# Graph layer on one Trainium2 core: where the first ranks, the first equality matrices, the early loads and the last list stand in a hand-ordered schedule

## Chip, cores and metric

The kernel runs on 1 core of one Trainium2 chip. The metric is the device time in microseconds (us) of one execution.

## The reference

200000 edges with 20 features each join 6250 nodes with 128 features. Cut to what is computed:

```python
h = relu(layernorm(x))                                   # 6250 x 128
xn = h @ W_in
W_ij = (softplus(f_ij @ W_f1 + b_f1) - log 2) @ W_f2 + b_f2   # one row for each edge
x_ij = xn[dst] * (W_ij * edge_weight1)                   # dst is sorted, src is not
out = segment_sum(x_ij, src, 6250)
return x + (softplus(out @ W_o1 + b_o1) - log 2) @ W_o2 + b_o2
```

The gather index (dst) is sorted, so neighbouring edges read neighbouring rows. The index of the sum (src) is not.

## The kernel before

The edges are cut into 391 quads of 512 edges. One quad is one **item** of the loop at line 1361. For each item PE multiplies the features (`s1_pe`, tile z), ACT takes exponential and logarithm (`s1_exp`, line 379, and `s1_ln`), DVE makes a one-hot matrix of the relative rows (`s1_oh`, line 391, from the tile rb, for two quads at a time), PE gathers node rows with it (`s2_pe_x`) and multiplies the second weights (`s2_pe_w`), ACT scales (`s2_copy`, line 572) and DVE multiplies the two (`s2_m`, line 582). Features are split into three bf16 parts on the chip, a block `fB[b]` of 4096 edges at a time (`fb_load`, `fb_1` to `fb_4`, and `fb_max`, which takes the block's largest value), and written to the DRAM tensor fsd. `load_sc(s)` reads ft from there for quads 2s and 2s+1, beside rb and the node rows wn. ft, rb and wn are loaded about four items ahead.

The products are summed by src in one of three ways:

- **Plain** quads (197 are not sorted; the first 12 of them and the last are plain): `s1_eq` compares the quad's src with itself into the tile eq, PE adds up equal rows with it (`s3_pe`), and four indirect DMAs with accumulation (**scatters**, line 644, issued by POOL) add the rows to an accumulator in DRAM. There are four accumulators, acc0 to acc3; `acc_of(k)` says which one scatter k goes to.
- **Listed** quads (the other unsorted ones): rows go out by scatters directly; rows whose src appears twice in a chunk are sent to rows of a list instead, and a window of 16 quads has one list of 128 rows. For each window, `l_eq`, `l_count` to `l_take` prepare the indices from tiles sb (four buffers); at its end `l_load` reads the list's rows from all four accumulators, `l_sum` (line 531) adds up equal ones on PE, and one scatter sends them.
- **Sorted** quads (every second item, 2, 4, ... 388): edges get a rank among those with the same 1/16 of the nodes (`rank_group` to `rank_slot`, eight quads at a time), one-hot matrices pm (`perm_oh`) permute the product's bf16 parts on PE (`permute`), ACT takes them to the tile sg (`perm_out`, line 766), SP sends sg into the tiles mst in another layout (`regroup`, line 773), and some items later **units** of 8 or 10 quads (`unit`, matmuls un of line 863) add them to accT, the transposed sums of all nodes in SBUF. `unit_evac` (line 879) adds PSUM to accT. What does not fit goes by an overflow row (`over_...`) with a scatter of its own.

eq and sg share one tag of three buffers. Each engine does its instructions in program order, and the order is written out by hand: `at(i, point, fn)` hangs a function on a point of item i, and the points (L, D0, D1, AX, DM, DR, PE2, D2, S and others) are run in the order of the loop's body. `put` takes offset and point from the table `AT`. SP issues most DMAs, also in this order.

Ahead of the loop stands a **prologue**: node group 0, block 0, items 0 and 1 whole, then `consts_late` (constants of the ranks, of the lists and of the overflow rows). Accumulators are zeroed in ten pieces each (`zero_piece`): acc0 and acc1 by POOL in the prologue, acc2 by SP in items 0 to 3 (Z2), acc3 by SP in items 14 to 41 (Z3). The second half of the relative rows is made by `half_load` and `half_piece` in items 1 to 5; items from 196 on read it.

Units are at items 24, 28, 32, 36, 40 and so on; the last four at 395, 397, 399 and 401. The last list starts at item 394 (`l_start`, then `over_row`, `l_load`, `l_sum`). Behind the loop come a check of flags, and a tail (lines 1511 to 1617) that reads acc1 to acc3, adds them and accT, and does the last two matrix products.

Of the kernel before, what the change touches and what calls it, by code (L numbers as in the profile page):

```python
# [7 lines left out]
F32 = mybir.dt.float32  # L8
BF16 = mybir.dt.bfloat16
I32 = mybir.dt.int32  # L10
# [3 lines left out]
ALU = mybir.AluOpType  # L14
AX = mybir.AxisListType
# [5 lines left out]
P = 128  # L21
SC = 1024
SEG = 512
# [46 lines left out]
CQ = 16  # L70
EARLY_N = 256
ZMAX = 60.0


@with_exitstack
def tile_gnn(ctx: ExitStack, tc: tile.TileContext, x, fB, cT, srcT, srcr, srci, dstr, win_, wf1, wf2, bias, bo1c, wo1,
# [20 lines left out]
    GN = NP // GRP  # L97
    ZR = 10 if ACC_R % 10 == 0 else 1
    ZEARLY = 3
    K1_END, K2_END, K3_END = 0, 12, 100  # L100
    Z2, Z3 = [0, 1, 1, 2, 2, 3, 3, 3, 3, 3], range(14, 44, 3)
    mpq = sorted_quads(NQ)
    mpi = {q: n for n, q in enumerate(mpq)}
    rounds = unit_rounds(mpq)
# [216 lines left out]
        fst[b]["f3"] = f3  # L321

    def fb_max(b):
        nc.vector.tensor_reduce(fmax[:, b:b + 1], fst[b]["f"], axis=AX.X, op=ALU.max, apply_absolute_value=True)

    def fb_2(b):
        fr = wk.tile([P, FE], F32, tag="fr", name="fr", bufs=1)
# [6 lines left out]
    def fb_4(b):  # L334
        f3 = fst[b]["f3"]
        nc.vector.tensor_tensor(f3[:, 2], fst[b]["fr"], f3[:, 1], op=ALU.subtract)
        nc.sync.dma_start(fsd[b].rearrange("g (p e) -> p g e", p=P), f3)
        del fst[b]

    def seg_of(s):  # L340
        return SEG if spread and s < HALF else WSEG
# [64 lines left out]
    def s1_eq(q):  # L406
        if not plainq(q):
            return
        n = plain[q]
        eq = wk.tile([P, 4, P], F32, tag="eq", name="eq", bufs=3)  # L410
        v = sbs[n // 2][:, n % 2 * SEG:(n % 2 + 1) * SEG]
        for b in range(2):
            nc.vector.tensor_tensor(eq[:, 2 * b:2 * b + 2],
                                    v[:, 2 * b * P:2 * (b + 1) * P].rearrange("p (i t) -> p t i", t=2),
                                    srcT_sb[:, n * 4 + 2 * b:n * 4 + 2 * b + 2].unsqueeze(2).to_broadcast([P, 2, P]),
                                    op=ALU.is_equal)
        st[q]["eq"] = eq
# [151 lines left out]
    def s2_copy(q):  # L569
        xc = wk.tile([P, 4, P], F32, tag="xc", name="xc")  # L570
        for c in range(4):
            nc.scalar.mul(xc[:, c, :], st[q]["xg"][:, c, :], late["c", q // CQ][:, 4 * (q % CQ) + c:4 * (q % CQ) + c + 1])  # L572
        st[q]["xc"] = xc

    def s2_m(q):
        if q in mpi:
            m = part_new(q)
        elif plainq(q):
            m = ms[plain[q] % 2]
        else:  # L580
            m = sp_.tile([P, 4, 132], F32, tag="s", name="s", bufs=6)
        nc.vector.tensor_tensor(m[:, :, :P], st[q]["W"], st[q]["xc"], op=ALU.mult)  # L582
        st[q]["m"] = m
# [82 lines left out]
    def rank_local(r):  # L666
        nc4 = rk[r]["n"]
        ext = exts[r % 2]
        nc.vector.scalar_tensor_tensor(ext[:, :nc4, 1], rk[r]["cnt"], float(-GN), rk[r]["srcf"], op0=ALU.mult,
                                       op1=ALU.add)  # L670
        nc.scalar.copy(ext[:, :nc4, 2], rk[r]["cnt"])
        rk[r]["ext"] = ext
# [254 lines left out]
    with tc.manual_schedule():  # L927
# [96 lines left out]
        iotl = cp.tile([P, P + LCAP], F16, name="iotl")  # L1024

        def consts_late():
            nc.vector.tensor_reduce(fmax[:, 0:1], fb0, axis=AX.X, op=ALU.max, apply_absolute_value=True)
            nc.vector.memset(onesf, 1.0)
            nc.vector.memset(dropT, 0.0)
            for ext_ in exts:  # L1030
                nc.vector.memset(ext_, 0.0)
            nc.vector.tensor_copy(wgtb, wgt)
            nc.vector.tensor_scalar(tri, iot[:, :P], lane, None, op0=ALU.is_gt)
            nc.vector.tensor_scalar(unit2[:, 0], iot[:, :P], lane, None, op0=ALU.is_equal)
            nc.vector.tensor_scalar(unit2[:, 1], iot[:, :P], lane, float(GN), op0=ALU.is_equal, op1=ALU.mult)
            nc.vector.tensor_scalar(trib, iot[:, :P], lane, float(BIG), op0=ALU.is_equal, op1=ALU.mult)
            nc.vector.tensor_tensor(trib, trib, tri, op=ALU.add)
            nc.vector.tensor_scalar(iotp, iot, float(BIG), None, op0=ALU.add)
            for mo_ in mos:
                nc.vector.tensor_copy(mo_[:, PW:PW + 1], wgt)  # L1040
            nc.vector.tensor_scalar(iotl, iotw[:, GN // 2:GN // 2 + P + LCAP], float(LCAP - 1), None, op0=ALU.subtract)
# [12 lines left out]
        def at(i, point, fn, *a):  # L1054
            hooks.setdefault((i, point), []).append((fn, a))

        def put(name, base, fn, *a, busy=()):
            d, point = AT[name]
            i = max(clear(base + d, busy) if busy else base + d, 0)
            at(i, point, fn, *a)  # L1060
            return i
# [2 lines left out]
            for fn, a in hooks.pop((i, point), []):  # L1064
                fn(*a)

        at(2 if spread else 0, "D2", rel_ext, 0, rel0)
        if CE < EP // P:
            w = (CE + 4 * NS) // 2
            for i, a, b in ((8, CE, w), (10, w, 4 * NS), (13, CB, EP // P)):  # L1070
# [4 lines left out]
            at(CQ * b - CQ // 2, "L", c_load, b)  # L1075

        def half_load(k):
            t_ = pg.tile([HALF, SEG], I32, tag="pm", name="half")
            nc.sync.dma_start(t_, dstr[HALF:2 * HALF, k * SEG:(k + 1) * SEG])
            idx[1, k * SEG] = t_  # L1080

# [2 lines left out]
            rel_ext(1 + k, rel(1, lo, hi, "x3", bufs=1))  # L1084

        for k in range(2):
            at(k + 1 if spread else 0, "L", half_load, k)
            at(2 * k + 3 if spread else 0, "D2", half_piece, k)
        for j in range(ZR):
            at(Z2[j] if spread else 0, "L", zero_piece, nc.sync, 2, j)  # L1090
        for j in range(ZR):
# [20 lines left out]
        for b in range(1, NB):  # L1112
            t0 = 2
            if b > 1:
                t0 = 8 * b - 8
                while t0 + 1 not in mpi or t0 + 1 in units:
                    t0 -= 1
                at(max(0, t0 - 6), "L", fb_load, b)
            if b > 1:
                put("fmax", t0, fb_max, b)  # L1120
            else:
                at(2, "D2", fb_max, b)
            put("f1", t0, fb_1, b)
            put("f2", t0, fb_2, b)
            put("f3", t0, fb_3, b)
            put("f4", t0, fb_4, b)
# [112 lines left out]
        for g in range(len(tgroups)):  # L1239
# [2 lines left out]
            at(i - 2, "L", r0_load, g)  # L1242
            at(i, "PE2", r0_tp, g)
            at(i + 1, "D0", r0_add, g)
        for r in range(-(-len(mpq) // RKQ)):
            i = mpq[RKQ * r]
            early = i < 8
            i = max(i, 4)
            put("rk_group", i, rank_group, r)
            put("rk_local", i, rank_local, r)  # L1250
            k = put("rk_count", i, rank_count, r, busy=units)
            k = max(k + 1, i + AT["rk_own"][0])
            at(k, AT["rk_own"][1], rank_own, r)
            k = clear(max(k, i + AT["rk_over"][0]), units)
            at(k, AT["rk_over"][1], rank_over, r)
            k = max(k + 1, i + AT["rk_slot"][0])
            assert k <= i + 1
            at(k, AT["rk_slot"][1], rank_slot, r)
# [3 lines left out]
        for w in range(NW):  # L1262
            for g in range(wsize[w] // 4):
                n = LB + SW * (w - 1) + 4 * g - LSHIFT
                i = splain[n] + 2 if w else 6 + 2 * g
                while w and (i not in mpi or i in units):
                    i -= 1
                for k in range(2):
                    kk = (LB + SW * w + 4 * g) // 2 + k
                    at(max(0, i + k - 2), "L", sb_load, kk)  # L1270
                    put("l_eq", i + k, l_eq, kk)
                i = put("l_count", i, l_count, (LB + SW * w) // 4 + g, busy=units)
                k = put("l_dup", i, l_dup, w, g)
            i = put("l_scan", i, l_scan, w)
            i = put("l_before", i - 1, l_before, w, busy=units)
            put("l_index", i, l_index, w)
            assert i + 1 <= splain[LB + SW * w] + 1
            put("l_id", i, l_id, w)
            i = put("l_place", i, l_place, w, busy=units)
            put("l_take", i, l_take, w)  # L1280
            i = clear(wend[w] + wlag[w], units)
            at(i, "L", l_start, w)
            put("l_dg", i, l_dg, w)
            at(i, "PE2", over_row, ("L", w))
            put("l_same", i, l_same, w)
            k = clear(i + AT["l_sum"][0], units)
            at(k - 1, "L", l_load, w)
            at(k, AT["l_sum"][1], l_sum, w)
            put("l_copy", k, l_copy, w)
            put("l_ji", k, l_ji, w)  # L1290
            k = put("l_int", k, over_int, ("L", w))
            at(k, "S", over_scatter, ("L", w))
# [51 lines left out]
            s1_ln(q)  # L1344
            s1_oh(q)
        for q in range(first):
            s1_eq(q)
            s2_pe_x(q)
            s2_pe_w(q)
            s2_copy(q)  # L1350
            s2_m(q)
        for q in range(first):
            s3_pe(q)
            s3_copy(q, 0)
            s3_copy(q, 1)
            s3_idx(q)
            s3_ji(q)
            s3_scatter(q)
        consts_late()
        s1_pe(first)  # L1360
        for i in range(max(NQ + 7, last + 22, r0_end + 2, lend + 24)):
            if i % 2 == 0 and i // 2 + 2 <= (NQ - 1) // 2:
# [301 lines left out]
def clear(i, busy, n=1):  # L1664
    while any(i + k in busy for k in range(n)):
        i += 1
    return i
# [114 lines left out]
```

## Time and profile before

| what | us |
|---|---|
| median of 3 runs | 1887.07 |
| lowest and highest of them | 1877.03, 1892.61 |
| the profiled execution | 1900.09 |
| its span | 1898.3 |
| mean granted TensorE clock, as a share of full speed | 0.963 |

Times in the profile count from the span's start. PE is TensorE's matmuls, PEld its weight loads, DVE VectorE, ACT ScalarE, POOL GpSimd, SP the engine that issues DMAs; SPq is its queue. A line of the timeline gives start, duration, engine, line of the kernel, operation, output and input, a count, and in brackets how long the engine had been idle and what ended that. A line of the waits gives who waited for whom: total, number of times, longest. Releasers are inferred.

### The profile page before, as it was taken

To read this page: it belongs to the slowest core of one execution; us is meant where nothing else is said; L and a number is where in the kernel's file an instruction comes from. 1 tells how busy PE (TensorE), PEld (TensorE's weight loads), DVE (VectorE), ACT (ScalarE), POOL (GpSimd) and SP (SyncE) were. 2 spreads that over 40 slices of the span, in tenths; PEclk is the share of its full clock that TensorE was granted. 3 is DMA by queue.
4 is the path that set the end of the run, shared out by engine and by line. 5 is a ranking of instruction groups with operands and counts; after the bars stand their busy time and mean duration, and the time that the engine had idled before them with its cause. 6 is when DMAs were issued, how large, how long until landed. Compare 5 with 4: busy or idle time off the path is not lost. (4 is left out here: it accounts for less than half of the span.)

```text
span 1898.3 us, 55497 instructions
## 1 busy us (share of the span) xinstructions
PE 1681.0 (89%) x19308; PEld 1122.6 (59%) x19308; DVE 1605.7 (85%) x4740; ACT 1471.1 (77%) x4068; POOL 1494.5 (79%) x949
## 2 busy tenths in 40 slices
PE   3769989999999999999999999999999999999746
PEld 2546655666666666666665566666666666666524
DVE  6678989899899989898899789889889899888636
ACT  4568878888788888887787788888888888888405
POOL 5557777888888888888888888888888888887845
PEclk8789999999999999999999999999999999999978
DMA  8878988888888888887887888888888888888647
GB/s 301 225 183 194 206 185 172 172 174 182 164 180 168 172 181 168 170 187 162 173 188 154 172 186 173 176 177 166 187 170 174 189 173 175 157 159 188 127 82 267
DMA packets 365471, 339.68 MB, mean 179 GB/s; under 512 B 86686, under 2 KB 328781, under 8 KB 365187
## 3 DMA queue, kind: packets, MB, share of 16 engines
q1 hardware_dynamic: 234005, 270.57, 49.1%
q0 software_dynamic: 130624, 65.33, 33.0%
q8 instruction: 152, 2.49, 0.6%
q14 instruction: 132, 1.08, 0.2%
q10 hardware_dynamic: 558, 0.20, 0.0%
HBM read 150.76 MB, written 108.08 MB: 136 GB/s over the span
## 5 line engine op out<-in xcount | busy, mean ns | idle before, releaser
L644 POOL DMA_INDIRECT acc<-s,lji x736 | 1188.0, 1614 | 245.1 <-issue 178.0
L572 ACT ACTIVATE xc<-xg,cb 128x128 f32<-128x128 f32 x1564 | 445.6, 371 | 16.9 <-PE xg L559 11.5
L567 PEld LDWEIGHTS W<-w,a 128*128 128x128 f32 x3128 | 428.7, 198 | 38.0 <-issue 24.7
L863 PE MATMUL un<-so,mst 32*128 32x392 bf16 x9312 | 433.9, 327 | 9.8 <-ACT sg L766 3.4
L567 PE MATMUL W<-w,a 128*128 128x128 f32 x3128 | 428.0, 281 | 0.1
L766 ACT CAST sg<-pq 128x388 bf16<-128x388 f32 x776 | 345.7, 493 | 84.6 <-DMA mst<-sg 45.4
L758 PE MATMUL pq<-pt,pm 128*128 128x388 bf16 x1552 | 333.4, 338 | 33.2 <-issue 9.1
L863 PEld LDWEIGHTS <-mst 32*128 32x128 bf16 x9312 | 232.8, 93 | 159.6 <-issue 19.0
L384 ACT ACTIVATE a<-a,con 128x512 f32<-128x512 f32 x391 | 282.4, 722 | 11.6
L379 ACT ACTIVATE a<-z 128x512 f32<-128x512 f32 x391 | 241.3, 617 | 39.1 <-PE z L374 34.1
L746 DVE TENSOR_TENSOR pt<-pt 128x512 f32<-128x512 f32 x388 | 264.1, 681 | 0.0
L879 DVE TENSOR_TENSOR accT<-un,accT 128x392 f32<-128x392 f32 x368 | 182.3, 557 | 68.0 <-PE z L374 42.5
L758 PEld LDWEIGHTS <-pm 128*128 128x128 bf16 x1552 | 147.3, 97 | 148.0 <-issue 58.0
L845 DVE TENSOR_SCALAR so<-iot,mst 128x392 bf16<-128x392 f16 x776 | 220.1, 334 | 8.6 <-PE un L863 7.1
L644 POOL DMA_INDIRECT acc<-os,oji x109 | 174.6, 1602 | 45.4 <-issue 17.0
L732 DVE TENSOR_SCALAR pm<-iotp,pos 128x384 bf16<-128x384 f16 x776 | 204.3, 324 | 0.0
L374 PE MATMUL z<-ft,ws 123*128 123x512 bf16 x391 | 155.0, 397 | 38.8 <-DMA ft<-fsd 11.1
L582 DVE TENSOR_TENSOR s<-W,xc 128x512 f32<-128x512 f32 x184 | 125.9, 684 | 70.7 <-issue 39.0
L582 DVE TENSOR_TENSOR pt<-W,xc 128x512 f32<-128x512 f32 x194 | 132.5, 683 | 47.4 <-ACT xc L572 31.0
L559 PE MATMUL xg<-wn,oh 63*128 63x128 bf16 x1564 | 157.1, 222 | 15.0 <-DVE oh L391 11.4
L556 PE MATMUL W<-b2rep,onesb 64*128 64x512 bf16 x391 | 154.5, 395 | 0.0
L781 PE MATMUL po<-pt,pm 128*128 128x387 bf16 x776 | 152.8, 338 | 1.3 <-DVE pt L746 0.7
(214 smaller groups left out, 1845.1 us busy)
## 6 DMA issues: line engine op xcount, KB each, us to landing
mst<-sg SPq DMA_DIRECT2D x776, 97.0 KB
sb<-src SPq DMA_DIRECT2D x98, 256.0 KB
rb<-reld SPq DMA_DIRECT2D x194, 128.0 KB
fsd<-f SPq DMA_DIRECT2D x49, 480.0 KB
ft<-fsd SPq DMA_DIRECT2D x96, 240.0 KB
fb<-in_fB_dram SPq DMA_DIRECT2D x49, 320.0 KB
ft<-fsd SPq DMA_DIRECT2D x96, 160.0 KB
acc<-s,lji POOLq DMA_INDIRECT x736
```

The costliest lines, as they stand in the source:

```text
L379: nc.scalar.activation(a, st[q]["z"], AF.Exp)
L384: nc.scalar.activation(a, a, AF.Ln, bias=half, scale=0.5)
L567: nc.tensor.matmul(W[:, c, :], st[q]["a"][:, c * P:(c + 1) * P], w2, start=False, stop=(c == 3))
L572: nc.scalar.mul(xc[:, c, :], st[q]["xg"][:, c, :], late["c", q // CQ][:, 4 * (q % CQ) + c:4 * (q % CQ) + c + 1])
L582: nc.vector.tensor_tensor(m[:, :, :P], st[q]["W"], st[q]["xc"], op=ALU.mult)
L644: nc.gpsimd.indirect_dma_start(out=accs[k][:rows, :], out_offset=bass.IndirectOffsetOnAxis(ap=ji, axis=0), in_=s, in_offset=None, compute_ ...
L732: nc.vector.tensor_scalar(pm[:, c], iotp, rk[r]["pos"][:, 4 * j + c:4 * j + c + 1], None, op0=ALU.is_equal)
L746: nc.vector.tensor_tensor(pt[:, :, k * P:(k + 1) * P], a, high(a), op=ALU.subtract)
L758: nc.tensor.matmul(t[:, :MW], mp[q]["pm"][:, c, s * P:(s + 1) * P], high(mp[q]["pt"][:, c:c + 1, :MW])[:, 0], start=(c == 2 * h), stop=(c ...
L766: nc.scalar.copy(mp[q]["sg", h][:, s], mp[q].pop(("q", k))[:, :MW])
L845: nc.vector.tensor_scalar(so, iotw[:, :GN], w[:, 3 * P // 2:3 * P // 2 + 1], None, op0=ALU.is_equal)
L863: nc.tensor.matmul(ts[g][:, :GN], mp[q]["ms", s // 2][v, s % 2, k * P:(k + 1) * P], mp[q]["oh"][v], start=(q == qs[0] and k == 0), stop=(q ...
```

## The change

- **Equality matrices**: the first 12 plain quads write eq into slices of accT instead of a buffer that sg shares.
- **First ranks**: `rank_group(0)` to `rank_slot(0)` move from the first items into the prologue, and `consts_late`, which they need, ahead of the products of items 0 and 1; in the prologue all products now stand ahead of the comparisons.
- **Late constants**: what the ranks don't need is split off as `consts_later` and done in item 5; `rel_ext(0)` moves from item 2 to 6, `fb_max(1)` from 2 to 7, other early `fb_max` to item 8 or later, `fb_load(2)` from 1 to 6.
- **Late index rows**: `half_load` and `half_piece` move to items 64, 67, 72 and 75, and their tile to the tag of the list's rows.
- **Zeros**: one piece of acc2 in each of items 0 to 9; scatters up to number 15 instead of 11 use acc0 and acc1 alone.
- **First list window**: its groups stand three items apart from item 7, not two from item 6.
- **Last list**: it starts behind the last unit, at item 402.

```diff
+HALF_AT = 64
...
-    K1_END, K2_END, K3_END = 0, 12, 100
-    Z2, Z3 = [0, 1, 1, 2, 2, 3, 3, 3, 3, 3], range(14, 44, 3)
+    K1_END, K2_END, K3_END = 0, 16, 100
+    Z2, Z3 = range(ZR), range(14, 14 + 3 * ZR, 3)
...
     def fb_max(b):
-        nc.vector.tensor_reduce(fmax[:, b:b + 1], fst[b]["f"], axis=AX.X, op=ALU.max, apply_absolute_value=True)
+        nc.vector.tensor_reduce(fmax[:, b:b + 1], fst[b]["f"] if b in fst else late["fb"], axis=AX.X, op=ALU.max, apply_absolute_value=True)
...
-        del fst[b]
+        late["fb"] = fst.pop(b)["f"]
...
-        eq = wk.tile([P, 4, P], F32, tag="eq", name="eq", bufs=3)
+        if n < min(LB, NP // SEG):
+            eq = accT[:, n * SEG:(n + 1) * SEG].rearrange("p (c f) -> p c f", c=4)
+        else:
+            eq = wk.tile([P, 4, P], F32, tag="eq", name="eq", bufs=3)
...
         def consts_late():
-            (fmax of block 0, onesf, wgtb, unit2, mos, iotl)
...
+        def consts_later():
+            (the same)
...
-        at(2 if spread else 0, "D2", rel_ext, 0, rel0)
+        at(6 if spread else 0, "D2", rel_ext, 0, rel0)
+        at(5 if spread else 0, "D2", consts_later)
...
-            t_ = pg.tile([HALF, SEG], I32, tag="pm", name="half")
+            t_ = wk.tile([HALF, SEG], I32, tag="lm", name="half", bufs=2)
...
-            at(k + 1 if spread else 0, "L", half_load, k)
-            at(2 * k + 3 if spread else 0, "D2", half_piece, k)
+            at(HALF_AT + 8 * k if spread else 0, "L", half_load, k)
+            at(HALF_AT + 8 * k + 3 if spread else 0, "D2", half_piece, k)
...
-                at(max(0, t0 - 6), "L", fb_load, b)
+                at(max(6, t0 - 6), "L", fb_load, b)
...
-                put("fmax", t0, fb_max, b)
+                at(max(8, t0 + AT["fmax"][0]), AT["fmax"][1], fb_max, b)
...
-                at(2, "D2", fb_max, b)
+                at(7, "D2", fb_max, b)
...
-        for r in range(-(-len(mpq) // RKQ)):
+        for r in range(1 if min(2, NQ) and spread else 0, -(-len(mpq) // RKQ)):
...
-                i = splain[n] + 2 if w else 6 + 2 * g
+                i = splain[n] + 2 if w else 7 + 3 * g
...
-            i = clear(wend[w] + wlag[w], units)
+            i = clear(max(wend[w] + wlag[w], uslots[-1][-1] + 1 if w == NW - 1 else 0), units)
...
         for q in range(first):
-            s1_eq(q)
             s2_pe_x(q)
             s2_pe_w(q)
             s2_copy(q)
+        consts_late()
+        if first and mpq:
+            rank_group(0)
+            rank_local(0)
+        for q in range(first):
             s2_m(q)
+        if first and mpq:
+            rank_count(0)
+        for q in range(first):
+            s1_eq(q)
+        if first and mpq:
+            rank_own(0)
...
-        consts_late()
+        if first and mpq:
+            rank_over(0)
+            rank_slot(0)
         s1_pe(first)
```

More of the change, by code (lines that the diff above doesn't have):

```diff
@@ L1026, in consts_late @@
         def consts_late():
-            nc.vector.tensor_reduce(fmax[:, 0:1], fb0, axis=AX.X, op=ALU.max, apply_absolute_value=True)
-            nc.vector.memset(onesf, 1.0)
             nc.vector.memset(dropT, 0.0)
@@ L1031, in consts_late @@
                 nc.vector.memset(ext_, 0.0)
-            nc.vector.tensor_copy(wgtb, wgt)
             nc.vector.tensor_scalar(tri, iot[:, :P], lane, None, op0=ALU.is_gt)
-            nc.vector.tensor_scalar(unit2[:, 0], iot[:, :P], lane, None, op0=ALU.is_equal)
-            nc.vector.tensor_scalar(unit2[:, 1], iot[:, :P], lane, float(GN), op0=ALU.is_equal, op1=ALU.mult)
             nc.vector.tensor_scalar(trib, iot[:, :P], lane, float(BIG), op0=ALU.is_equal, op1=ALU.mult)
@@ L1038, in consts_late @@
             nc.vector.tensor_scalar(iotp, iot, float(BIG), None, op0=ALU.add)
+        def consts_later():
+            nc.vector.tensor_reduce(fmax[:, 0:1], fb0, axis=AX.X, op=ALU.max, apply_absolute_value=True)
+            nc.vector.memset(onesf, 1.0)
+            nc.vector.tensor_copy(wgtb, wgt)
+            nc.vector.tensor_scalar(unit2[:, 0], iot[:, :P], lane, None, op0=ALU.is_equal)
+            nc.vector.tensor_scalar(unit2[:, 1], iot[:, :P], lane, float(GN), op0=ALU.is_equal, op1=ALU.mult)
             for mo_ in mos:
```

## The prediction

> **What bounds the kernel now.** I read the busy shares first, then POOL alone, since its instructions are the scatters into the accumulators.
>
> ```profile
> PE 1681.0 (89%) x19308; PEld 1122.6 (59%) x19308; DVE 1605.7 (85%) x4740; ACT 1471.1 (77%) x4068; POOL 1494.5 (79%) x949
> 36.00:164.60 128.60, 74.50 (x44) 0.82 0.84 219
> 164.60:291.00 126.40, 92.42 (x58) 1.00 0.87 192
> 291.00:1818.00 1527.00, 1272.46 (x790) 0.98 0.84 171
> 285.03 1.54 POOL L644 DMA_INDIRECT acc<-s,lji  x1 [0.30 <-issue]
> 290.59 1.56 POOL L644 DMA_INDIRECT acc<-s,lji  x1 [4.02 <-DVE lsel L490]
> ```
>
> By the first row PE looks like the bound. The three scatter rows (stretch, its length, POOL's busy time in scatters with their count, granted clock, DMA share, GB/s) say otherwise. A scatter is followed by a gap of 0.30 us even when nothing holds it. From 291 to 1818 us, 790 scatters of 1272.46/790 = 1.611 us and 790 x 0.30 = 237 us of gaps fill 1509 of 1527 us. POOL is the bound there, and its last long wait ends at 290.59. Before that it starves: 44 scatters in 128.6 us. So only two places can move the time: how early the items up to about 290 us feed POOL, and what follows POOL's last scatters.
>
> The items' pace is read from one instruction per item, the exponential of line 379 (items 2, 8, 17, 24, 40), and from the stages between (busy time of PE, its weight loads, DVE, ACT, POOL, then clock, DMA share, GB/s):
>
> ```profile
> 28.62 0.58 ACT L379 ACTIVATE a<-z 128x512 f32<-128x512 f32 x1
> 69.20 0.61 ACT L379 ACTIVATE a<-z 128x512 f32<-128x512 f32 x1
> 127.83 0.65 ACT L379 ACTIVATE a<-z 128x512 f32<-128x512 f32 x1
> 164.64 0.69 ACT L379 ACTIVATE a<-z 128x512 f32<-128x512 f32 x1
> 232.06 0.61 ACT L379 ACTIVATE a<-z 128x512 f32<-128x512 f32 x1
> 28.60:60.00 31.40, 16.68 (x88) 11.78 (x88) 24.78 (x72) 16.54 (x42) 17.46 (x17) 0.62 0.98 314
> 60.00:127.80 67.80, 46.26 (x327) 32.55 (x328) 40.51 (x120) 39.05 (x114) 36.13 (x22) 0.82 0.82 211
> 127.80:164.60 36.80, 28.77 (x216) 20.69 (x213) 29.87 (x101) 30.24 (x88) 26.32 (x17) 0.95 0.79 177
> 164.60:232.00 67.40, 65.15 (x786) 43.20 (x785) 62.29 (x182) 59.49 (x168) 51.99 (x32) 1.00 0.88 193
> ```
>
> Items 24 to 40 take 67.4/16 = 4.2 us each; items 2 to 24 take 136/22 = 6.2 us. DMA is at 0.98 up to 60 us and near 0.8 after it: the first stage is short of transfers, the next two mostly wait on each other:
>
> ```profile
> ACT sg L766 <- DMA mst<-sg: 24.5, 8, 8.5
> POOL acc L644 <- ACT ji L625: 29.8, 7, 8.8
> DVE eq L413 <- DMA sb<-src: 5.7, 1, 5.7
> SPq L400 <- DVE eql L427: 8.4, 2, 5.1
> SPq L355 <- DMA fsd<-f: 5.1, 1, 5.1
> ```
>
> **The change, the end first.** The last list's work moves from item 394 to item 402, behind the last four units.
>
> ```profile
> 1814.69 1.54 POOL L644 DMA_INDIRECT acc<-s,lji  x1 [0.30 <-DMA acc<-s,lji]
> 1817.98 1.29 SPq L513 DMA_DIRECT2D lm<-acc  x3
> 1796.36 0.49 PE L531 MATMUL lsum<-lm,leq 128*128 128x128 f32 x2 [0.83 <-DVE accT L879]
> 1820.12 1.74 PE L531 MATMUL lsum<-lm,leq 128*128 128x128 f32 x6 [23.27 <-DMA lm<-acc]
> 1822.35 7.17 PE L863 MATMUL un<-so,mst 32*128 32x392 bf16 x120
> 1840.78 5.13 PE L863 MATMUL un<-so,mst 32*128 32x392 bf16 x117 [0.15 <-DVE accT L879]
> 1845.80 1.98 DVE L879 TENSOR_TENSOR accT<-un,accT 128x392 f32<-128x392 f32 x4 [2.95 <-PE un L863]
> 1823.93 1.54 POOL L644 DMA_INDIRECT acc<-os,oji  x1 [0.30 <-issue]
> 1849.09 11.24 SPq L1521 DMA_DIRECT2D ta_in<-acc  x18
> 1800.00:1820.00 20.00, 0.00 (x0) 0.00 (x0) 0.00 (x0) 0.00 (x0) 16.88 (x11) 0.50 0.43 42
> ```
>
> The list's sum on PE waits 23.27 us for rows that cannot be read until the list's last scatter (1814.69) has landed. Queued behind it on PE stand three units, which need no scatter; they run from 1822.35 to the evacuation's end at 1847.78, 25.4 us, and the tail's loads follow at 1849.09. After the change the units start where the sum waited, 1796.4, and are evacuated by 1821.8. The sum then runs with its rows there: 2 us of matmuls, then copy, index and integer, about 1826. POOL reaches it third after 1823.93, at 1.85 us each: 1827.6, ends 1829.2. The list's own scatter needed 1817.98 - 1816.23 = 1.75 us to land, so loads start near 1831. In 1800 to 1820 POOL ran its 1.54 us with all else idle; beside work it is 1.611, so 17 scatters cost 1.2 us more: 1832. Gain **17 us**. If each unit took 3.6 us (half of 7.17) longer, they would be evacuated at 1832.6, chain, scatter and landing would take 7.5 more, and the gain would be 9. With no lengthening it is 19. What waits behind the list's chain now is only the tail. The loads of x leave their place behind the list's loads on SP, and the additions of line 1212 fall beside the units.
>
> The granted clock fell to 0.50 while PE stood, and the unit went from 7.17 to 5.13 us as it recovered. The Trainium skill, "TensorE: Matmul & The Clock Gate", section "What's actually happening", says that an idle window halves the clock and sustained work restores it; the rows agree. By that rule, the units, now without the stall ahead of them, would end some 6 us sooner; POOL would still end last, and the total falls by about 1 us.
>
> **The prologue.** Four kinds of edit work on the same stretch.
>
> ```profile
> 28.30 0.81 DVE L1027 TENSOR_REDUCE fmax<-fb 128x1 f32<-128x640 f32 x1
> 34.66 0.18 DVE L702 TENSOR_SCALAR ov<-rank 128x32 bf16<-128x32 f32 x1
> 43.12 0.23 DVE L977 TENSOR_SCALAR base_i<-half,con 98x2 int32<-98x2 int32 x1 [2.15 <-DMA half<-in_dstr_dram]
> 45.12 0.68 DVE L990 TENSOR_REDUCE ext<-rel_f 98x1 f32<-98x512 f32 x1
> 44.00 5.38 SPq L202 DMA_DIRECT2D acc<-zero  x7
> 52.03 0.39 SPq L337 DMA_DIRECT2D fsd<-f  x1
> 62.82 0.59 PE L374 MATMUL z<-ft,ws 123*128 123x512 bf16 x1 [2.90 <-DMA ft<-fsd]
> 44.04 1.57 POOL L644 DMA_INDIRECT acc<-s,ji  x1 [6.47 <-DMA acc<-zero]
> 72.82 1.54 POOL L644 DMA_INDIRECT acc<-s,ji  x1 [0.30 <-issue]
> 58.17 4.00 POOL L644 DMA_INDIRECT acc<-s,ji  x1 [0.79 <-DMA acc<-s,ji]
> ```
>
> First, items 2 to 8. Constants and first ranks hold DVE from 28.30 to 34.84, and item 2's comparison stands behind them. Most of them (about 4 us) move into DVE's 5.7 us wait for sb; were that cover gone, they would cost those 4 us. A half piece takes DVE 43.12 to 45.80, after a wait of 2.15, and 5 zero pieces in one item hold SP (seven issues with other zeros, 5.38 us); both stand ahead of the write of fsd at 52.03, on which ft and item 8's matmul (62.82) wait. Without them that write could go out some 10 us sooner. But DMA was at 0.98: what leaves the stretch is two half loads (98 x 512 x 4 bytes each), as much again at two bytes written back and three of ten zero pieces (128 x 640 x 4 bytes), 1.6 MB, at 314 GB/s 5 us; the 5.1 us in which SP waited for fsd, with DMA draining, overlaps the rest. I take 9, bounds 4 and 13.
>
> Second, items 8 to 17. With the equality matrices in accT, which no unit writes until item 25, sg has three buffers to itself: a buffer comes back after three items instead of two. The first list's loads, two in three items instead of two in two, take SP's 8.4 us of waits away. All sg waits gone would give 24.5 us. DMA caps that: 67.8 x 0.82 = 55.6 us of transfer, plus 3 us for the three zero pieces that come here, less 1.6 for two sb loads that leave, is 57; at the 0.88 of the stage that runs at pace, 65 us, a gain of 3; at 0.98, a gain of 9.6. I take 5, bounds 0 and 10, nearer the 0.88. Third, items 17 to 24: 36.8 x 0.79 + 1.6 = 30.7, at 0.88 35: gain 2, bounds 0 and 5.
>
> Sum **16**, bounds 4 and 28. POOL allows it: the first scatter into the second accumulator still waits for its zeros (44.04); ten more came by 72.82, 2.62 us apart (two accumulators, each waiting for the other's landing). Two accumulators until scatter 16 put it at 44 + 14 x 2.62 = 81, and 28 more at 1.693 + 0.30 end at 137 against 164: room for 27. Scatters 13 to 16 may pay 5 us for having two accumulators instead of three; POOL waits 29.8 us for indices there, which hides it.
>
> The moved half pieces now cost DVE 2 x 2.7 us and SP four issues at items 64 to 75, where POOL has a backlog of up to six s tiles (24 scatters, 46 us): nothing; without backlog, at most 5.4 + 2 x 2.15 = 10. Maxima and late constants move between idle places of DVE (24.78 busy in 31.4): nothing, at most 3. The profiled execution took 1900.09 (span 1898.3), so it would be 1867. It lies 13 us above the median of its runs; the savings carry over: 1887.07 - 33 = **1854**.
>
> **Rivals.** (a) The prologue is hidden by transfers: DMA keeps its 0.8, the three buffers only move the wait from sg to ft or rb; for it speaks 0.98 up to 60 us, against it the 24.5 us of sg waits at 0.82. Only the tail gains: 1870. (b) The waits all go and POOL's 27 is the limit, with the first stage's bound: 17 + 27, and a little less tail: about 1843. (c) The tail doesn't do what it says: the units wait for inputs of their own, not for the sum, and end as late as now, with the list's chain behind them. The price: chain, scatter and landing, 7.5 us, follow 1847.78, 6 us later than now, so 1887 - 16 + 6 = 1877. Against it: un starts at once when the list's matmuls end. (d) Slower: POOL's scatters lengthen in the long stage, since everything there is their number times their length. 790 x 0.042 us eat the gain, so from a mean of 1.653 on it is lost; at the 1.693 of the first stage it is 790 x 0.082 = 65 us, 1919. For it: single scatters of 4.00 us beside DVE work (58.17), and a change of the items' phase against POOL. Against it: no work of that stage changes but two half pieces. The Trainium skill, "SBUF — State Buffer", section "SBUF: two separate sides", has such a mechanism: while VectorE runs an operation on both its port pairs, GpSimd cannot write descriptors. The trace agrees only in part: 1.54 with DVE idle, 1.611 beside it.
>
> **Numbers.** Forecast 0.62, with its own range 1838 to 1868; (a) 0.17; (b) 0.10; (c) 0.07; (d) 0.04. The range 1830 to 1873 takes in the forecast, (a) and nearly all of (b), the prologue's bounds with the tail's 9 to 19 among them, and leaves out (c) and (d). 1% is 18.9 us, about what a measurement of this kernel can tell from no change: faster than 1868 are nearly all of the forecast and (b), and half of (a): 0.80; same 0.16, slower 0.04.
>
> **What would show it.** No wait of PE for lm and none of 20 us anywhere near the end; tail loads within 3 us of the last scatter's end, some 49 us before the last instruction; item 8's exponential near 60 and item 24's near 149; waits of sg for mst under 8 us; POOL 99% full from about 275 on. I am wrong if item 24 stays at 160 or later, if the mean scatter leaves 1.60 to 1.63, or if the units end after POOL.

## The result, and the profile after

The kernel after took **1863.86 us** (median of 5 runs, 1863.70 to 1870.14), the one before 1886.43 (5 runs): a ratio of 0.9899, 95% interval 0.9874 to 0.9923, or 19 us with 14 to 24. Two later comparisons of the same pair gave 0.9853 (0.9825 to 0.9880) and 0.9865 (0.9841 to 0.9890), 28 and 26 us. The forecast was 1854 and 33 us: the sign and the range were right, both terms too large. The profiled execution of after took 1863.70 (span 1861.9).

The end first, of the kernel after: units and the list's sum on PE, two of POOL's last three scatters, and SP's loads of rows and of the tail (start, duration, what, and in brackets the idle time before with its releaser).

```profile
1760.76 7.97 PE L867 MATMUL un<-so,mst 32*128 32x392 bf16 x118 [1.53 <-DVE accT L1199]
1770.64 5.13 PE L867 MATMUL un<-so,mst 32*128 32x392 bf16 x117 [0.15 <-DVE accT L883]
1784.76 5.13 PE L867 MATMUL un<-so,mst 32*128 32x392 bf16 x117 [0.15 <-DVE accT L883]
1798.31 1.29 SPq L517 DMA_DIRECT2D lm<-acc  x3
1800.34 1.84 PE L535 MATMUL lsum<-lm,leq 128*128 128x128 f32 x6 [7.17 <-DMA lm<-acc]
1804.19 1.99 POOL L648 DMA_INDIRECT acc<-os,oji  x1 [0.32 <-issue]
1808.32 1.54 POOL L648 DMA_INDIRECT acc<-os,oji  x1 [0.30 <-DMA acc<-os,oji]
1812.46 17.54 SPq L1540 DMA_DIRECT2D ta_in<-acc  x28
```

All units are done by 1790, ahead of the list. The sum's wait for its rows is 7.17 us where it was 23.27. The tail's loads start 2.6 us after the last scatter's end and 49.4 us before the span's end. From the third-to-last scatter to these loads it took 8.27 us, where it was 25.16.

Then the items: exponentials of items 2, 8, 17 and 24, the stages between them (busy time of PE, its weight loads, DVE, ACT, POOL, then granted clock, DMA share, GB/s), the long stage's scatters, and three of the largest waits from 20 to 180 us (us, times, longest; a landing is the end of a transfer).

```profile
29.44 0.58 ACT L380 ACTIVATE a<-z 128x512 f32<-128x512 f32 x1
66.02 0.65 ACT L380 ACTIVATE a<-z 128x512 f32<-128x512 f32 x1
114.11 0.60 ACT L380 ACTIVATE a<-z 128x512 f32<-128x512 f32 x1
150.83 0.64 ACT L380 ACTIVATE a<-z 128x512 f32<-128x512 f32 x1
60.00:114.00 54.00, 37.77 (x285) 27.67 (x285) 38.89 (x107) 38.73 (x113) 30.44 (x17) 0.84 0.91 245
114.00:150.80 36.80, 30.78 (x222) 22.79 (x222) 31.72 (x109) 30.33 (x88) 28.50 (x17) 0.86 0.95 223
278.00:1798.00 1520.00, 1266.13 (x790) 0.99 0.84 174
POOL acc L648 <- DMA acc<-s,ji: 23.3, 19, 3.3
ACT sg L770 <- DMA mst<-sg: 12.6, 5, 4.4
ACT f L321 <- DMA fb<-in_fB_dram: 11.9, 2, 10.0
```

Item 24 comes 13.8 us earlier (164.64 before), but item 8 only 3.2. The DMA share rose from 0.82 and 0.79 to 0.91 and 0.95: what was a chain of waits now looks short of transfers (e9 below tests it). ACT's wait for a block of the features is new, and POOL's for landings with two accumulators has grown from 9.6 to 23.3 us; POOL's 29.8 us for indices are gone.

### The profile page after: what moved, and what is told of

The parts are those of the page before. It is cut to its first block, busy times and chain, and to the rows that moved or that the text cites. A ratio compares the mean times of both kernels' runs of the same rounds, so it can differ in the third digit from the quotient of the medians.

```text
span 1861.9 us, 55503 instructions
## 1 busy us (share of the span) xinstructions
PE 1663.2 (89%) x19308; PEld 1114.3 (60%) x19308; DVE 1612.2 (87%) x4740; ACT 1466.1 (79%) x4068; POOL 1486.0 (80%) x949
## 4 chain that ended last, share of the span: by engine, by line
PE 36%; DVE 28%; DMA 12%; ACT 11%; issue 6%; SPq 4%; POOL 3%; DVEq 0%; ACTq 0%; POOLq 0%
PE un L867 10%; PE W L571 8%; PE pq L762 6%; DMA mst<-sg 5%; PE po L785 5%; DVE pt L750 4%; DVE accT L883 4%; ACT sg L770 4%; PE z L375 3%; DVE pm L736 3%; POOL acc L648 3%; ACT xc L576 3%; DVE s L586 2%; DMA acc<-s,lji 2%; DMA ft<-fsd 2%
## 5 line engine op out<-in xcount | busy, mean ns | idle before, releaser
L762 PE MATMUL pq<-pt,pm 128*128 128x388 bf16 x1552 | 328.3, 335 | 29.5 <-ACT mo L790 9.6
L385 ACT ACTIVATE a<-a,con 128x512 f32<-128x512 f32 x391 | 282.4, 722 | 11.6
L736 DVE TENSOR_SCALAR pm<-iotp,pos 128x384 bf16<-128x384 f16 x776 | 208.9, 329 | 0.0
L563 PE MATMUL xg<-wn,oh 63*128 63x128 bf16 x1564 | 156.5, 221 | 12.1 <-DVE oh L392 10.6
```

Source lines behind the costliest of these rows:

```text
L385: nc.scalar.activation(a, a, AF.Ln, bias=half, scale=0.5)
L736: nc.vector.tensor_scalar(pm[:, c], iotp, rk[r]["pos"][:, 4 * j + c:4 * j + c + 1], None, op0=ALU.is_equal)
L762: nc.tensor.matmul(t[:, :MW], mp[q]["pm"][:, c, s * P:(s + 1) * P], high(mp[q]["pt"][:, c:c + 1, :MW])[:, 0], start=(c == 2 * h), stop=(c ...
```

## The experiments

Three sets ran, each beside its own runs of the kernel before, whose medians were 1887.29 us (24 runs; e1 to e4), 1902.01 (11; e5, e6, e7 and e9) and 1898.09 (12; e8 and e10 to e12); so ratios are compared, and the unchanged kernel after stood in the second and third set.

| kernel | median us (runs) | ratio to before, 95% interval |
|---|---|---|
| e1_tail_only | 1873.30 (7) | 0.9943, 0.9921 to 0.9964 |
| e2_prologue_only | 1878.69 (12) | 0.9957, 0.9942 to 0.9972 |
| e3_before_again | 1883.81 (10) | 0.9985, 0.9966 to 1.0004 |
| e4_fb_early | 1869.83 (6) | 0.9908, 0.9884 to 0.9931 |
| e5_after_again | 1873.03 (6) | 0.9853, 0.9825 to 0.9880 |
| e6_third_acc_12 | 1875.52 (6) | 0.9858, 0.9827 to 0.9889 |
| e7_eq_shared | 1879.30 (6) | 0.9883, 0.9850 to 0.9916 |
| e9_zeros_late | 1872.98 (6) | 0.9854, 0.9824 to 0.9884 |
| e8_half_early | 1873.00 (6) | 0.9876, 0.9846 to 0.9905 |
| e10_all_early | 1865.54 (5) | 0.9826, 0.9800 to 0.9851 |
| e11_fewer_scatters | 1880.52 (5) | 0.9917, 0.9884 to 0.9949 |
| e12_after_third | 1872.47 (6) | 0.9865, 0.9841 to 0.9890 |

**The two halves by themselves.** The first is the kernel before with one line changed, the second the kernel after with that line as it was; the third is before, for a second profile.

```diff
-            i = clear(wend[w] + wlag[w], units)
+            i = clear(max(wend[w] + wlag[w], uslots[-1][-1] + 1 if w == NW - 1 else 0), units)
```

> The kernel before with the last-list edit alone. Theory: the tail gains what the pair of traces shows between the third-to-last scatter and the tail loads, 25.2 against 8.3 us, so 17 us (bounds 9 to 19): a ratio of 0.991, and the tail loads within 3 us of the last scatter's end. Rival (the prologue carries the 22.6 us of the medians, the tail less): under 10 us, a ratio above 0.9947.

> The kernel after with its last list put back where it was, so the prologue's edits alone. Theory: what the medians leave beside the tail, 22.6 - 17 = 6 us, a ratio near 0.997. Rival (the items' times of the pair of traces hold, 13 to 14 us): a ratio near 0.993. In both the tail shows the 20-us wait for lm again.

> The kernel before unchanged, for a second profile of it: ratio 1.00. Theory (the first profiled run of 1900.1 us was a long sample): a span near 1885, the gap to the first profile spread over the long stage or in the prologue, so that item 24's exp starts earlier than 164.6 or the scatters' mean is under 1.611 us. Rival: the same prologue and the same long stage, with a span near 1898.

The tail alone is worth 0.57% of 1887.29, 10.8 us (6.8 to 14.9), the prologue alone 0.43%, 8.1 us (5.3 to 10.9). My theory for the tail said 17, the rival under 10: the measurement lies between them. So does the prologue's 0.9957, between 0.997 and 0.993. The unchanged kernel's second profile has a span of 1882.2, 16 us shorter than the first, with item 24 no earlier (165.72), but scatter 500 to 600 took 190.3 us against 197.0 and the tail was shorter. So the first profile lost its time in the long stage and at the end, not in the prologue. Its last scatters and tail loads, then those of the tail alone; the scatter of the first row of each pair has 22 others before that of the second:

```profile
1768.18 1.54 POOL L644 DMA_INDIRECT acc<-os,oji  x1 [0.33 <-issue]
1810.80 1.54 POOL L644 DMA_INDIRECT acc<-os,oji  x1 [0.42 <-issue]
1832.43 17.33 SPq L1521 DMA_DIRECT2D ta_in<-acc  x27
```

```profile
1763.78 1.98 POOL L644 DMA_INDIRECT acc<-os,oji  x1 [0.30 <-ACT ojd L796]
1809.70 1.98 POOL L644 DMA_INDIRECT acc<-os,oji  x1 [0.30 <-issue]
1817.84 19.26 SPq L1521 DMA_DIRECT2D ta_in<-acc  x30
```

From the start of the third-to-last scatter (the second row) to the loads: 21.63 us, against 8.14. That is a gain of 13.5. But the 23 steps before it took 42.62 us and now take 45.92: 3.3 us are paid back, because the units now run while POOL still scatters. Two of POOL's waits from 1762 to 1812 us, in the tail alone (in e3, without the edit, all its gaps there are of 0.30 to 0.42 us):

```profile
POOL acc L644 <- DMA acc<-s,lji: 1.8, 2, 0.9
POOL acc L644 <- DVE so L845: 1.4, 1, 1.4
```

Net 10.2 in this pair; in the prologue alone against after, 65.50 and 54.10 us from the same scatter to the loads, 11.4.

The short end is not there in every execution. In e5, the kernel after once more, the last scatter waits for its own list, whose sum now stands behind the units; in e9 and in e11 (both below) it waits longer:

```profile
1817.24 2.01 POOL L648 DMA_INDIRECT acc<-os,oji  x1 [4.35 <-DVE xl L1219]
1811.47 2.01 POOL L648 DMA_INDIRECT acc<-os,oji  x1 [6.52 <-DVE xl L1219]
1824.32 2.01 POOL L648 DMA_INDIRECT acc<-os,oji  x1 [20.20 <-DVE xl L1219]
```

The releaser named is an addition that stands behind the list's index on DVE; the chain that ended last runs through the units, the list's sum and its index. So from the third-to-last scatter to the loads it took 8.27, 12.22 and 8.05 us in the three profiles of the kernel after (after, e5, e12). In four of the eleven profiles with the moved list (e5, e9, e10, e11) the units and the list end behind POOL's other scatters.

**What holds the prologue.**

> The kernel after with fb_load for the third block issued from item 3 on instead of item 6, and the first block's maximum moved from the later constants back among the late ones. If the 10.0-us wait of ACT for fb is on the path of items 7 to 24: 3 to 6 us faster than after (a ratio to before near 0.987), and item 8's exp near 61 instead of 66.0. If the transfers of the prologue (busy share 0.91 to 0.95) set its pace: item 8 earlier, item 24 near 150 as in after, and the time within 2 us of after's.

```diff
...
-                at(max(6, t0 - 6), "L", fb_load, b)
+                at(max(3, t0 - 6), "L", fb_load, b)
```

> The kernel after with transfers moved out of items 9 to 24: the three zero transfers of each of the first three lists, 768 KB a list, at items 17, 20, 23 instead of 9, 11, 13, and the ten zero pieces of the fourth accumulator, 320 KB each, at items 24 to 42 instead of 14 to 41. Theory (transfers are the bound there): 2.3 MB at 245 GB/s and more are 8 to 9 us, so item 15's exp comes 4 to 9 us earlier than 102.3 and item 24's 2 to 6 earlier than 150.8. Whether that reaches the end is a second question: if POOL can follow, the time falls by 2 to 5 us against after; if POOL, which waits for landings there, can't, the lead is gone by scatter 115 and the time is that of after within 1.5 us.

```diff
-LZERO = (9, 11, 13, 41)
+LZERO = (17, 20, 23, 41)
-    Z2, Z3 = range(ZR), range(14, 14 + 3 * ZR, 3)
+    Z2, Z3 = range(ZR), range(24, 24 + 2 * ZR, 2)
```

The exponentials tell what each did (us; e5 and e12 are the kernel after; e7, e8 and e10 are described below):

| item | e3 (before) | after | e5 | e12 | e4 | e9 | e8 | e7 | e10 |
|---|---|---|---|---|---|---|---|---|---|
| 6 | 51.29 | 41.09 | 40.38 | 40.15 | 39.07 | 40.42 | 50.33 | 41.22 | 42.60 |
| 8 | 67.48 | 66.02 | 65.91 | 66.06 | 56.70 | 64.51 | 67.59 | 65.82 | 61.15 |
| 13 | 108.04 | 86.78 | 88.16 | 87.18 | 84.53 | 85.19 | 88.15 | 95.01 | 83.97 |
| 15 | 118.24 | 102.31 | 102.89 | 104.25 | 99.98 | 94.05 | 104.81 | 106.62 | 95.09 |
| 24 | 165.72 | 150.83 | 148.57 | 150.98 | 145.43 | 140.86 | 151.13 | 152.57 | 140.92 |

Without the wait for fb, item 8 comes 9 us earlier, but item 15 only 2.3 and item 24 5.4; the ratio, 0.9908, is no better than after's 0.9899 (the kernel after did not stand in e4's set). With 2.3 MB of zeros and the fourth accumulator's moved out, items 15 and 24 come 8 to 10 us earlier than in the three profiles of after: the transfers set the pace there. And the time is again after's, 0.9854 beside 0.9853: by the medians, no more of the items' lead in the prologue reaches the end. In e9's profile, its fastest run, POOL does carry it there: the third-to-last scatter starts at 1801.56 us, earlier than in all three of after (1804.19, 1809.50, 1813.15). The wait of 6.52 us for the list behind the units then puts the tail's loads at 1815.97, between the 1812.46 and the 1821.72 of after and e5.

**Two terms by themselves.**

> The kernel after with the half pieces at items 1 to 5 and the first index rows at item 2 again, as before the change. The prediction gave items 2 to 8 a gain of 9 us, most of it from this. If that is so: item 8's exp 5 us or more later than in after (66.0), scatter 115 (starting at 304.3 in after) 4 to 9 later, the time 4 us or more above after's. If the transfers of items 9 to 24 swallow it: item 24 within 3 us of after's 150.8 and the time within 2 us.

```diff
...
-            at(HALF_AT + 8 * k if spread else 0, "L", half_load, k)
-            at(HALF_AT + 8 * k + 3 if spread else 0, "D2", half_piece, k)
+            at(k + 1 if spread else 0, "L", half_load, k)
+            at(2 * k + 3 if spread else 0, "D2", half_piece, k)
```

The half pieces early cost item 6 10 us, item 8 1.5 and item 24 nothing (151.13 against 150.98); the time is 0.5 us from e12's. What the prediction took for most of its first term fills a wait that is there anyway: ACT's wait for the block, from 40 to 80 us first in e8, then in e12 (where it is put down to a transfer queued beside it), is 6.5 us shorter with the half pieces ahead of it.

```profile
ACT f L321 <- DMA fb<-in_fB_dram: 4.4, 1, 4.4
```

```profile
ACT f L321 <- DMA mst<-sg: 10.9, 1, 10.9
```

> The kernel after with the equality matrices back in the buffers that they shared with sg. The prediction gave items 8 to 17 a gain of 5 us, for the most part from this. Theory (transfers, at a share of 0.91 to 0.95, set the pace of these items): the waits of sg for mst rise from 12.6 to 20 us or more, item 24's exp comes 0 to 3 us later than 150.8, and the time is within 2 us of after's. Rival (the buffers set the pace): item 24 at 156 or later and the time 4 us or more above after's.

```diff
-        if n < min(LB, NP // SEG):
+        if n < 0:
```

Item 13 is 7 us later than in e5, item 24 4.0, the time 6.3 us longer by the medians; but the two intervals overlap, and the waits of sg are 11.6 us, not the 20 that I expected. So the matrices' place is worth about 4 us at item 24, of the 5 that were given to it; whether all of it reaches the end is not settled.

**POOL's own lead.**

> The kernel after with the third accumulator in use from scatter 12 as before, not from 16. In after POOL waits 23 us for landings between items 2 and 24. If those waits are what keeps POOL from following the items: scatter 16 some 3 to 5 us earlier than in after, and 2 to 4 us off the time (a ratio near 0.988). If they are hidden by later waits, as the prediction had it: the same time as after, within 1 us, though scatters 12 to 15 come closer together.

```diff
-    K1_END, K2_END, K3_END = 0, 16, 100
+    K1_END, K2_END, K3_END = 0, 12, 100
```

POOL does come forward: the twentieth scatter starts at 93.34 us, against 101.71, 97.10 and 101.96 in the three profiles of after, the hundredth 7.2 us ahead of e5's. At the 401st it is 5.6 ahead, at the 501st 0.4, and the time is after's. Where the lead goes, from 640 to 980 us, first e6, then e5:

```profile
POOL acc L648 <- ACT pt L756: 6.5, 3, 2.9
POOL acc L648 <- DVE accT L883: 3.2, 10, 0.5
```

```profile
POOL acc L648 <- DMA acc<-s,lji: 2.6, 8, 0.5
POOL acc L648 <- DVE accT L883: 1.4, 2, 1.1
```

In e6 POOL stands three times, 6.5 us in all, for ACT's work on the items, by the releaser that the profile infers; in e5's list no such wait stands. That fits a POOL that has caught up with its supplier.

**Is POOL the bound of the long stage?** One kernel leaves 45 of its scatters out.

> The kernel after without 45 of the list scatters, the first of four in every third such item from the sixtieth plain item on; those rows are missing from the sums. At 1.60 us and a gap of 0.30 they are 86 us of POOL. As the prediction has it (POOL is the bound from 291 to 1818 us, everything else follows): 60 to 86 us off. Theory (the items' own pace lies only a few us behind POOL's): 8 to 25 us off, with POOL waiting for items where it now only has its 0.30-us gaps.

```diff
-            for c in range(nchunks(q)):
+            for c in range(1 if plain[q] % 3 == 2 and plain[q] >= 60 else 0, nchunks(q)):
                 scatter(st[q]["m"][:, c, :P], lst["ji", w][:, 4 * k + c:4 * k + c + 1], l_base(w) + P)
```

It was not a microsecond faster: 1880.52 beside 1872.47. The long stage (busy PE, weight loads, DVE, ACT, POOL, clock, DMA) and POOL's waits in it, first with fewer scatters, then the kernel after of the same set:

```profile
278.00:1700.00 1422.00, 1331.66 (x15712) 881.82 (x15703) 1271.40 (x3781) 1184.65 (x3295) 1142.65 (x707) 0.99 0.83 172
POOL acc L648 <- DVE s L586: 42.4, 33, 4.3
POOL acc L648 <- ACT pt L756: 29.0, 19, 3.9
```

```profile
278.00:1700.00 1422.00, 1331.84 (x15746) 884.03 (x15738) 1270.92 (x3782) 1185.20 (x3299) 1191.70 (x736) 0.99 0.84 174
POOL acc L648 <- DVE s L586: 3.7, 12, 0.3
```

In the same 1422 us PE did the same work, 1331.7 us or 93.6%, and the time that POOL was spared became waits for the items. Their pace is their own: item 380 comes at 1716.83 and 1714.46. My 8 to 25 us were wrong too. POOL alone is not the bound of the kernel after: its third-to-last scatter starts at 1791.53 us, 21.6 us before e12's, and then it waits 9.51 us for an overflow row's index and 20.20 us for the list behind the units. Which engine sets the items' pace is not shown: PE is the busiest, DVE stands at 1270.9 us or 89.4%, and no kernel here takes work from either.

The 8 us by which it was slower come at the end: from 1717 to 1790 us PE ran fewer matmuls, at a lower clock, first here, then in after:

```profile
1717.00:1790.00 73.00, 60.87 (x633) 42.90 (x636) 48.84 (x142) 43.37 (x123) 51.46 (x34) 0.89 0.74 149
```

```profile
1717.00:1790.00 73.00, 64.21 (x808) 44.42 (x807) 55.14 (x162) 41.47 (x120) 57.68 (x37) 0.98 0.84 183
```

Matmuls of one shape took longer there: the products `po` 394 ns against 333, `W` of line 571 303 against 277. PE waited 1.62 us for an earlier list's rows at 1751.88 us, and the granted clock from 1752 to 1757 was 0.58, where e12 has 1.00; whether that is the whole cause is not shown.

**Both at once.**

> The kernel after with three edits at once: fb_load from item 3, third accumulator from scatter 12, the zeros of the first three lists at items 17, 20, 23 and of the fourth accumulator at items 24 to 42. Theory (two bounds lie close together, the items' own pace and POOL's; an edit that moves only one of them loses its lead at the other): now both lead, item 24's exp at 136 to 142, scatter 115 5 to 10 us earlier than in after, and 4 to 8 us of it reach the end, a ratio 0.002 to 0.004 under after's. Rival (the rest of the prologue's lead is lost in the long stage whatever it is): the time of after within 2 us.

It has the edits of e4, e6 and e9 together. Item 24 comes at 140.92, the hundredth scatter at 267.71 against 276.20 in e12 (268.74 in e5) and the 851st at 1721.42 against 1728.74 (1723.99). All five runs (1864.41 to 1869.25) lie under all six of after (1869.82 to 1876.16): 7 us by the medians, 0.9826 beside 0.9865, though the two intervals just overlap. The edits, none of which was worth anything alone, are worth some 7 us together, as the theory forecast. That this is because both chains lead is argued: no kernel has two of the three edits, and the profile, of the slowest of the five runs, loses 4.12 us of its lead to the list at the end. This is the fastest version of the study.

> The kernel after unchanged, timed beside the others on one chip. Theory (the edits add up: tail alone 0.9943, prologue alone 0.9957): a ratio of 0.990, so 19 us. Rival (the first comparison, 22.6 us by the medians, holds): 0.988.

> The kernel after unchanged, so that the three others have it beside them in the same session: a ratio between 0.985 and 0.990, as in the two sessions before.

Neither of the two expectations of e5 came out: 0.9853 is below both. That of e12 did. The change is worth 19 to 28 us, more in the sets in which the kernel before was slower.

## Why the prediction was right or wrong

**Right.** The list behind the units does what it says: no 20-us wait near the end, the loads 2.6 us behind the last scatter, 49 us before the end. The scatters' mean stayed, 1266.13/790 = 1.603 us, and no wait of POOL from 278.06 us to its last scatter is over 2.4 us, so rival (d) was off. The units start 1.5 us after their place in the order comes, so (c) was off in this profile; in e5 the list behind the units ends last, as (c) and the last sign of being wrong had it, but that costs 4.35 us. Rival (a) was half right in its reason, as transfers do bind the prologue now, but at 0.91 to 0.95 and not at 0.8. Item 24 moved by 13.8 of the 16 us. On the clock the Trainium skill's rule ("TensorE: Matmul & The Clock Gate", section "What's actually happening") agrees with the rows as weighed there: with no 20-us stall ahead of them three of the four units run at 5.13 us in the profile of after, and POOL still ends last there, so the total gains little from it. In e12 a shorter stall was enough: the granted clock was 0.50 from 1793.37 to 1796.78 us, and the third unit took 6.81 us, though in the 3.41 us before PE was busy for 2.05 and its longest wait was 0.91 us. The slower matmuls of e11, whose PE idled more, agree as well.

**Luck in the total.** Both terms came out near half their size or little above it: 10.8 and 8.1 us, in sum 18.9. Taken from 1887 that is 1868, the upper end of the forecast's own range; the two later medians of after, beside slower runs of before, are 1873.03 and 1872.47.

**Wrong, the tail: 17, measured 10.8.** The term "17 scatters cost 1.2 us more" was mis-sized: the scatters that now run beside the units cost 3.3, in waits for landings and behind DVE's work on the units. And the wait that was removed came from one execution: 25.16 us from the third-to-last scatter to the loads, where two other profiles of the same tail have 21.63 and 22.92. Their mean of 23.2, less 8.2, less 3.3 is 11.7; with 9.2, the mean of four ends after the change (8.14, 8.27, 12.22 and 8.05), it is 10.7.

**Wrong, the prologue's parts: 9, 5 and 2, in the traces about 0 to 4, 10 to 13 and 0 to 3.** From item 2 to 8 it took 40.58 and 36.44 us before, 36.58 after. Item 8 was to come near 60 and came at 66: the edit that I had costed at nothing, the later load of fb, put a 10-us wait where the half pieces had stood.

```profile
63.49 0.72 ACT L321 CAST f<-fb 128x640 bf16<-128x640 f32 x1 [9.98 <-DMA fb<-in_fB_dram]
```

From item 8 to 17, 58.63 and 59.88 us became 48.09, above the upper bound of 10. There the mis-sized term is the 57 us of transfers. From 60 us to item 17's exponential the DMA engines were busy 49 to 50 us in the three profiles of after, at shares of 0.90 to 0.95; at the 0.88 that was taken, 49 to 50 us give a gain of 11 to 12. Which transfers left the stage is not shown.

**Wrong, from the items to the end: 16, measured 8.1.** The step was "POOL is the bound there" with "POOL allows it ... room for 27". Of the items' lead of 15.5 us at item 24 (e2 against e3) POOL had 10.6 at the hundredth scatter, 8.6 at the 287th and 6.6 at the 871st. Item 380 still came 13 us earlier in this pair, but it comes at 1701.36, 1720.17 and 1714.46 us in the three profiles of after, so one pair says little about it. POOL's scatters are one chain, the items another, and in the kernel after they run at nearly one pace: POOL with gaps of hardly more than 0.30 us, PE busy 93.6%. The end gains what the slower of the two gains. The room was also read too wide: from 44.04 to 72.82 us there are ten steps of 2.88 us, not 2.62, which puts scatter 16 at 84 and leaves 24 (in the profiles of after it starts at 84 to 88). Scatters 13 to 16 with two accumulators did pay, about 4 to 9 us of POOL's time; "hidden" was right for the sum, but by the items, not by the waits for indices.

**The frame.** "It lies 13 us above the median of its runs; the savings carry over" took the terms of a long execution for those of the median one. Some of its length was in the tail wait itself.

## What to carry to other kernels

An engine without gaps is not yet the only bound: look at the busy share of what feeds it, and ask how far the queue between them lets one run ahead. A lead given to one of two chains that run at one pace can be worth nothing until the other has it too; a kernel that leaves some of one engine's work out shows at once whether that engine alone is the bound. Work that is moved to the end brings its own chain with it, and that chain can end last. A wait that is to be removed is sized from more than one profile, and what the moved work takes from the engine it now runs beside is subtracted.

## What was not expected of the hardware

The unchanged kernel before had medians of 1887.29 (24 runs) and 1902.01 (11 runs) on the same chip in two sets, 0.8% apart, while the intervals within each set reach about a quarter per cent either way. The change's ratio moved with it, 0.9899 in one comparison and 0.9853 in another. A difference under 1% is to be read only beside the other kernel in the same set; that is why two experiments needed the unchanged kernel after beside them.
